# A decoder layer on one core: convolution results stored in one DMA a group, constant key rows written in the front, the loop's first tiles on other memory, two gates placed behind the convolution

## The chip, the cores and the metric

One core of a Trainium2 chip runs the whole kernel. The metric is the device time of one execution in microseconds (us): 2160.04 us, the median of three runs.

## The reference

x is 16 sequences of 512 tokens with 256 channels, the context 16 x 64 x 128. One decoder layer is three blocks, each `x = layernorm(x + block(x))`. Cut to what matters:

```python
# block 1: a gated long convolution, then a gated MLP
z = rmsnorm(u, pre_norm_w) @ in_proj_w.T                 # (16, 512, 768)
z = causal_conv3(z, short_w) + short_b                   # each channel by itself, 3 taps
x2, x1, v = split(z, 3)                                  # x2 is "the gate"
h = sum_s residues * exp(log_poles * t)                  # 256 long filters, 16 poles each
xv = x1 * v
y = (causal_conv(xv, h) + xv * D_skip) * x2
y = y @ out_proj_w.T + u
block1 = y + (gelu(rms(y) @ l1_w.T) * (rms(y) @ l2_w.T)) @ l3_w.T
# block 2: 16 heads of causal self-attention plus cross-attention to the context
block2 = (softmax(causal(q k.T)) v + softmax(qc kc.T) vc) @ Wp + bp
# block 3: a low-rank feed-forward
block3 = gelu(x @ U1 @ V1 + b1) @ U2 @ V2 + b2
```

## The kernel before

All matmuls are in float32. The kernel has two parts, each an ordered list of operations that a planner writes: `Plan.op` takes an operation with its engine, a cost, a priority, the tiles it reads and writes and the operations it must follow; `Plan.schedule` simulates the engines with those costs, picks by priority whatever can start, and `emit` writes the instructions in that order. Each engine then runs its own instructions in order, and so does the sync engine's DMA queue, which before the change issues every DMA. Buffers of a class (`"x"`: 10 tiles fx, `"row"`: 9 tiles frow, `"mm"`: the PSUM banks, ...) are given out by the same planner, and an operation that finds none waits.

**The front** (lines 362 to 920) makes what the long convolution needs of all 16 batches. `prepare(b)` loads x of a batch (L439), takes the sum of squares on ACT (L317), the inverse root on POOL (L306, L307), scales x on POOL (`scale_ops`, L330) and transposes it on PE (L344). `project(m)` is two matmuls (L469, four instructions in the trace), an activation (L476) and two multiply-adds on DVE (L484) for the three taps. `x1v(b, k)` makes two projections, multiplies them on POOL (L496), transposes the product (L502) and puts it into `xv0` or `xv1` (channels 0 to 127 and 128 to 255). `gate_of(b)` makes the two gate projections and stores them to the DRAM tensor `gates` (L518). The second half of the channels and the gates of the last nine batches come late; the gates of the last two batches (`LAST`) have the lowest priority. A transposed x stays in its fx tile until the gate of its batch is done.

The convolution then goes in eight blocks of 32 channels, four on `xv0` and four on `xv1`. A block loads four Toeplitz tiles ("toes", 512 KB each, into fx tiles, L641), which POOL cuts to a triangle (L650), and runs `near_mm` (L665), the state (L675, L685, L693), `toe_mm` (L716), ACT's exps into the single tile `far` (L701) and `far_mm` (L728). Four results of 128 x 512 are copied to rows by ACT or DVE (L297, L299) and stored to `yconv` in DRAM, each by two DMAs of 64 partitions (L746).

Weights are loaded in between, and biases and weights folded (L832, L878). The front's memory is then given to the pool `kept` of the second part. A tile of `kept` waits for whatever last used the memory it lies on (`reuse_waits="tile"`). In the order of the pool's list, `xt`, `yt`, `gate` and `y1` lie on `xv0`; `xT`, `gT` and the first rows on `xv1`; `va` lies on `far` and the first frow tiles.

**Between the two parts** POOL fills `va`, `vc`, `maxes` with constants (L958 to L971) and two row tiles are made (L966, L967) and stored into the DRAM tiles `dk` (L969): constant rows beside the keys.

**The loop** plans all 16 batches together: `first_block(b)` loads x (L1056), the gate (L1053) and the two halves of the convolution's result (`load_y`, L1047), multiplies by the gate on POOL (L1065), projects out (L1078), adds (L1028), takes the rms norm (L317, L306, L332), adds y to x on POOL (L1090), transposes (L344) and runs the MLP (L1103 onwards, L1155, additions at L1163); `attention(b)` and `ffn(b)` follow. While one batch is in attention, the next is in its MLP.

Of the kernel before, what the change touches and what calls it, by code (L numbers as in the profile page):

```python
# [8 lines left out]
F32 = mybir.dt.float32  # L9
# [7 lines left out]
P = 128  # L17
NEG = -1.0e30
HEADS = 16
# [178 lines left out]
def decoder_layer(  # L198
# [69 lines left out]
    hpad = dram.tile([D + 1, P], F32, name="hpad")  # L268
    yconv = dram.tile([NT, B, D, P], F32, name="yconv")
    gates = dram.tile([B, P, KD * T], F32, name="gates")  # L270
    normed = dram.tile([B, P, KD * T], F32, name="normed")
    weights = ctx.enter_context(tc.tile_pool(name="weights", bufs=1))
# [16 lines left out]
    def pool_(n):  # L289
        return 0.2 + n / 470.0  # L290
# [34 lines left out]
    def scale_ops(x, sq, prio, on):  # L325
        for c in range(NT):

            def fn(e, c=c):
                if e == "POOL":
                    nc.gpsimd.tensor_scalar(x.t[:, c, :], x.t[:, c, :], sq.t[:, c, 8:9], None, ALU.mult)  # L330
                else:
                    nc.scalar.activation(x.t[:, c, :], x.t[:, c, :], AF.Copy, scale=sq.t[:, c, 8:9])  # L332

            plan.op(on, pool_(D) if on == "POOL" else act(D, True), fn, prio, r=[sq], w=[(x, c)])

# [28 lines left out]
    with ExitStack() as front:  # L364
# [69 lines left out]
        def prepare(b, pr):  # L434

            x_ = View("x", lambda t: t.rearrange("p (c d) -> p c d", c=NT))
            plan.op(
                "SP", 0.5 * MB,
                lambda e: nc.sync.dma_start(out=x_.t, in_=x[b].rearrange("(c p) d -> p c d", p=P)), pr - 1000,  # L439
                w=[x_], lat=2.5, after=at_step(b - 3),  # L440
            )
            if b == 0:
                load_in(prew, pre_w, -900, [(INW, "p")])
                for k in range(KD):
                    load_in(inw[:, k, :], in_wT[bass.ts(k, P), :], -900, [(INW, k)])
                load_in(cw, conv_w, -890, [(CW, 0)])
                load_in(cb, conv_b, -890, [(CW, 1)])
                for k in range(KD):
                    plan.op(
                        "DVE", 0.9,  # L450
                        lambda e, k=k: nc.vector.tensor_scalar(
                            inw[:, k, :], inw[:, k, :], prew[:, k : k + 1], None, ALU.mult
                        ),
                        -900, r=[(INW, "p")], w=[(INW, k)],
                    )

            sq = rms_ops(x_, pr - 120)
            scale_ops(x_, sq, pr - 120, "POOL")
            xT = transposed(x_, lambda t: t, pr - 120, as_xT())
            marks.append(plan.ops[-1])  # L460
            return xT

        def project(m, xT, pr):

# [7 lines left out]

            plan.op("PE", KD * pe(T), mm, pr + 10, r=[xT, INW], w=[ps], holds=[t])
            plan.op(
# [37 lines left out]

        def gate_of(b, xT, pr):
            for m in range(KD):
                t = project(m, xT, pr)
                plan.op(
                    "SP", 0.25 * MB,
                    lambda e, m=m, t=t: nc.sync.dma_start(out=gates[b][:, bass.ts(m, T)], in_=t.t), pr,  # L518
                    r=[t], lat=2.5,
                )  # L520

        late, late_T = [], []
        for b in range(B):
# [15 lines left out]
        for b, xT in late:  # L539
# [12 lines left out]
            if b < B - LAST:  # L552
                gate_of(b, xT, 3000 + b * 100)
        for b, xT in late_T[LATE - LAST :]:
            gate_of(b, xT, 7000 + b * 100)

# [72 lines left out]
        for blk in range(NR // R8):  # L629
# [102 lines left out]

            plan.op("PE", 1.0, far_mm, pc + 10, r=[st, far], w=ys, tiling=(SLOT, P // 2))
            for c in range(HPG):
# [7 lines left out]
                )  # L742
                for par in range(2):
                    plan.op(
                        "SP", 0.6,
                        lambda e, c=c, o=o, par=par, d0=d0: nc.sync.dma_start(  # L746
                            out=yconv.rearrange("j b d t -> (j b) d t")[
                                :, d0 + c * R8 + par * R8 // 2 : d0 + c * R8 + (par + 1) * R8 // 2, :
                            ],
                            in_=o.t[bass.ts(par, 64)],  # L750
                        ),
                        pc + 10, r=[o], lat=3.0,
                    )

# [104 lines left out]
        for par in range(2):  # L859
            for rows_, col in (  # L860
# [6 lines left out]
                ones_.append(t)  # L867


        bias_p = load(bp.to_broadcast([P, D]), [P, D], "bias_p")  # L870
# [60 lines left out]
        "mm": tiles(psum, "mm", 3, [P, T]),  # L931
        "xt": tiles(kept, "xt", 5, [P, NT, D]),
        "yt": tiles(kept, "yt", 1, [P, KD, T]),
        "gate": tiles(kept, "gate", 1, [P, KD * T]),
        "y1": tiles(kept, "y1", 1, [P, NT, D]),
        "xT": tiles(kept, "xT", 3, [P, KD, T]),
        "gT": tiles(kept, "gT", 1, [P, NF, T]),
# [5 lines left out]
        "ctx2": tiles(kept, "ctx2", 2, [CC, 2, TC]),  # L943
        "va": tiles(kept, "va", 2, [P, NT, VA]),
        "vc": tiles(kept, "vc", 2, [P, HEADS // 2, SLOT]),
        "maxes": tiles(kept, "maxes", 2, [P, NT, HPG, SLOT]),
        "ex": tiles(kept, "ex", 3, [P, HPG * T]),
# [3 lines left out]
        "di": tiles(dram, "di", 2, [2 * HPG, 2, T]),  # L951
        "dk": tiles(dram, "dk", 2, [2 * HPG, SLOT, T]),
        "junk": tiles(kept, "junk", 1, [P, D]),
# [6 lines left out]
    for t in pool["vc"]:  # L960
        nc.gpsimd.memset(t, 0.0)
        nc.gpsimd.memset(t[:, :, 0:1], 1.0)

    for par in range(2):
        fixed = pool["row"][par]
        nc.gpsimd.memset(fixed, 0.0)  # L966
        nc.vector.tensor_scalar(fixed, fixed, first_rows[par], None, ALU.add)  # L967
        for t in pool["dk"]:
            nc.sync.dma_start(out=t[bass.ts(par, HPG), HD:, :], in_=fixed[0 : HPG * HD, :])  # L969
    for t in pool["maxes"]:  # L970
# [70 lines left out]
    def first_block(b, after):  # L1041
# [4 lines left out]
        def load_y(e, k):  # L1046
            nc.sync.dma_start(  # L1047
                out=yt.t[:, k, :].rearrange("p (j t) -> p j t", j=NT),
                in_=yconv[:, b, bass.ts(k, P), :].rearrange("j p t -> p j t"),
            )  # L1050
# [9 lines left out]
        for k in range(KD):  # L1060
            plan.op("SP", 0.5, lambda e, k=k: load_y(e, k), p0 - 500, w=[(yt, k)], lat=4.0)
        for k in range(KD):
            plan.op(
                "POOL", pool_(T),
                lambda e, k=k: nc.gpsimd.tensor_tensor(  # L1065
                    yt.t[:, k, :], yt.t[:, k, :], gate.t[:, bass.ts(k, T)], ALU.mult
                ),
                p0 - 100, r=[gate], w=[(yt, k)],
            )
# [16 lines left out]
        for cp in range(NT // 2):  # L1086
# [3 lines left out]
                lambda e, sl=sl: nc.gpsimd.tensor_tensor(x_.t[:, sl, :], x_.t[:, sl, :], y1.t[:, sl, :], ALU.add),  # L1090
                p0, r=[(y1, 2 * cp), (y1, 2 * cp + 1)], w=[(x_, 2 * cp), (x_, 2 * cp + 1)],
            )
# [707 lines left out]
```

## Time and profile before

| | |
|---|---|
| median of three runs (lowest, highest) | 2160.04 us (2159.8, 2162.32) |
| the profiled execution: its own time, and its span from first to last instruction | 2162.7 us, 2161.0 us |
| mean granted TensorE clock | 0.972 |
| DMA moved | 182.15 MB, mean 84 GB/s |
| DMAs in the front: yconv stores, gate stores, toes | 64 of 128 KB, 32 of 256 KB, 32 of 512 KB |

How to read it: PE, DVE, ACT and POOL are the tensor, vector, scalar and GpSimd engines; PEld is PE's weight load; SPq is the sync engine's DMA queue. A line of the timeline gives the start, the time from the first to the last of the merged instructions, engine, line, operation, output and input, their number, and in brackets the idle time before them and what ended it. A line of the windows gives a stretch, its length, the busy time of PE, PEld, DVE, ACT and POOL (with the number of instructions), the granted PE clock, the DMA share and GB/s. A line of the waits gives who waited for whom, the total, the number of times and the longest wait, in us.

### The profile page before, as it was taken

The page shows a single profiled execution, that of the slowest core. Times are in us where ns is not written, and L with a number is a line of the kernel's source. Part 1 is how long each engine was busy: PE and PEld are TensorE (multiplying, and loading weights), DVE is VectorE, ACT ScalarE, POOL GpSimd, SP SyncE. Part 2 cuts the span into 40 slices and gives each one's busy share as a digit, 9 for nine tenths or more (in the row PEclk, how much of TensorE's full clock was granted, in tenths as well). Part 3 has the DMA queues.
Part 4 walks back from the last instruction along what each step waited for, and adds up shares of the span by engine and source line. Part 5 has one row for each costly group of instructions (what it writes and reads, how often), then busy time and mean ns, then how long its engine had stood idle before and what let it go on. Part 6 is the DMA issues. An engine that isn't in the chain of part 4 may idle for free.

```text
span 2161.0 us, 35414 instructions
## 1 busy us (share of the span) xinstructions
PE 2028.3 (94%) x14324; PEld 1043.9 (48%) x14324; DVE 1342.1 (62%) x1928; ACT 941.8 (44%) x1381; POOL 720.6 (33%) x960
## 2 busy tenths in 40 slices
PE   7999949798999999999999999999999999999676
PEld 3555625444454545454545454545454545454232
DVE  5976513738384848484848484848485857575742
ACT  6863421060627161716171617161626262626243
POOL 7585432040414141414142414141414141313122
PEclk9999969899999999999999999999999999999889
DMA  5366861030304031413141313131313131212100
GB/s 177 108 203 223 260 176 49 1 109 21 110 21 125 25 119 31 119 31 119 31 118 32 117 34 114 36 114 36 113 38 110 41 96 45 76 45 75 56 10 10
DMA packets 114887, 182.15 MB, mean 84 GB/s; under 512 B 13346, under 2 KB 61987, under 8 KB 114595
## 3 DMA queue, kind: packets, MB, share of 16 engines
q1 hardware_dynamic: 114722, 179.88, 27.6%
q8 instruction: 113, 1.85, 0.4%
q14 instruction: 52, 0.42, 0.1%
HBM read 111.09 MB, written 68.76 MB: 83 GB/s over the span
## 4 chain that ended last, share of the span: by engine, by line
PE 80%; ACT 5%; DVE 4%; issue 2%; POOL 2%; DMA 1%; SPq 0%; ACTq 0%; POOLq 0%; DVEq 0%
PE mm L1103 13%; PE scores L1347 10%; PE mm L1256 8%; PE mm L1155 8%; PE scores L1425 7%; PE av L1460 7%; PE mm L1650 4%; PE av L1666 3%; PE mm L1184 3%; PE mm L1017 2%; PE fmm L469 2%; PE mm L344 2%; PE mm L1512 2%; ACT ex L1437 2%; PE scores L1486 2%
## 5 line engine op out<-in xcount | busy, mean ns | idle before, releaser
L1437 ACT ACTIVATE ex<-scores 128x2048 f32<-128x2048 f32 x160 | 300.1, 1876 | 175.5 <-PE scores L1425 172.9
L1103 PE MATMUL mm<-xT,w_l 128*128 128x512 f32 x640 | 296.6, 607 | 0.0
L1448 POOL TENSOR_SCALAR_AFFINE_SELECT ex<-ex 128x512 f32<-128x512 f32 x256 | 158.1, 635 | 381.9 <-ACT ex L1437 350.4
L1347 PE MATMUL scores<-keys,q 32*128 32x320 f32 (+4 forms) x2560 | 233.9, 472 | 42.9 <-DVE maxes L1377 18.3
L1366 DVE TENSOR_TENSOR scores<-scores,mask_qk 128x512 f32<-128x512 f32 (+1 forms) x192 | 168.3, 876 | 102.6 <-PE scores L1347 98.7
L1347 PEld LDWEIGHTS scores<-keys,q 32*128 32x128 f32 x2560 | 116.5, 191 | 179.0 <-issue 57.9
L1658 ACT ACTIVATE row<-mm,b_s 128x512 f32<-128x512 f32 x128 | 80.8, 684 | 254.0 <-PE mm L1650 253.9
L1425 PE MATMUL scores<-q,keys 32*128 32x512 f32 (+3 forms) x2048 | 183.1, 460 | 7.1 <-ACT ex L1437 7.0
L1103 PEld LDWEIGHTS mm<-xT,w_l 128*128 128x128 f32 x640 | 115.7, 190 | 146.3 <-issue 129.0
L1594 POOL TENSOR_TENSOR nd<-nd,nd 128x1024 f32<-128x1024 f32 x30 | 70.6, 2353 | 346.6 <-DMA nd<-di 346.6
L306 POOL TENSOR_SCALAR small<-small 128x4 f32<-128x4 f32 (+1 forms) x66 | 13.1, 199 | 517.2 <-DVE small L987 515.7
L1002 ACT ACTIVATE xt<-xt,small 128x256 f32<-128x256 f32 x192 | 102.7, 594 | 173.6 <-POOL small L995 144.4
L469 PE MATMUL fmm<-fx,inw 128*128 128x512 f32 x384 | 176.8, 605 | 0.0
L1460 PE MATMUL av<-ex,va 128*32 128x512 f32 (+3 forms) x2048 | 168.1, 439 | 0.0
L1115 ACT ACTIVATE row<-mm 128x512 f32<-128x512 f32 x80 | 47.8, 597 | 271.6 <-PE mm L1103 271.6
L484 DVE SCALAR_TENSOR_TENSOR frow<-fmm,cw,frow 128x511 f32<-128x511 f32 x192 | 140.6, 744 | 36.8 <-ACT frow L476 32.6
L297 DVE COPY row<-av 128x512 f32<-128x512 f32 x66 | 45.7, 692 | 184.0 <-PE av L1460 165.5
L1155 PE MATMUL mm<-w_l,gT 128*128 128x256 f32 x640 | 158.9, 384 | 0.0
L1379 DVE TENSOR_REDUCE maxes<-scores 128x4 f32<-128x2048 f32 x64 | 146.7, 2293 | 2.2
L1425 PEld LDWEIGHTS scores<-q,keys 32*128 32x128 f32 x2048 | 89.3, 183 | 104.4 <-ACT ex L1437 33.5
L1155 PEld LDWEIGHTS mm<-w_l,gT 128*128 128x128 f32 x640 | 117.9, 190 | 43.8 <-issue 30.3
L1262 DVE TENSOR_SCALAR q<-mm,bqc_s 128x512 f32<-128x512 f32 x63 | 47.3, 751 | 140.0 <-PE mm L1256 140.0
(178 smaller groups left out, 3339.8 us busy)
## 6 DMA issues: line engine op xcount, KB each, us to landing
dn<-row SPq DMA_DIRECT2D x120, 256.0 KB
fx<-hpad SPq DMA_DIRECT2D x32, 512.0 KB
keys<-dk SPq DMA_DIRECT2D x64, 256.0 KB
nd<-dn SPq DMA_DIRECT2D x30, 512.0 KB
nd<-di SPq DMA_DIRECT2D x30, 512.0 KB
fx<-in_x SPq DMA_DIRECT2D x16, 512.0 KB
gates<-frow SPq DMA_DIRECT2D x32, 256.0 KB
yconv<-frow SPq DMA_DIRECT2D x64, 128.0 KB
```

The costliest lines, as they stand in the source:

```text
L469: nc.tensor.matmul(ps.t, inw[:, k, bass.ts(m, P)], xT.t[:, k, :], start=(k == 0), stop=(k == KD - 1))
L484: lambda e, lag=lag: nc.vector.scalar_tensor_tensor(t.t[:, lag:], ps.t[:, 0 : T - lag], cw[:, m, 2 - lag : 3 - lag], t.t[:, lag:], ALU.mul ...
L1103: nc.tensor.matmul(ps.t, w[:, k, bass.ts(f, P)], zT.t[:, k, :], start=(k == 0), stop=(k == KD - 1))
L1155: nc.tensor.matmul(ps.t[:, bass.ts(cc, D)], gT.t[:, f, bass.ts(c, P)] if f < NF else gE.t, w_l3[:, f, :] if f < NF else w_l3e[:, c, :], st ...
L1256: nc.tensor.matmul(ps.t, w[:, k, cols], xT.t[:, k, :], start=(k == 0), stop=(k == KD - 1))
L1347: nc.tensor.matmul(sc.t[:, r, at : at + hi - lo], q.t[hd, bass.ts(i, P)], kk.t[hd, lo:hi], start=True, stop=True,)
L1366: nc.vector.tensor_tensor(diag, diag, mask, ALU.add)
L1379: nc.vector.tensor_reduce(own[:, 3], sc.t, AX.X, ALU.max, negate=True)
L1425: nc.tensor.matmul(sc.t[:, r, at : at + T - j * P], keys[g].t[hd, TC + j * P : TC + (j + 1) * P], qas[g].t[hd, j * P :], start=True, stop= ...
L1437: lambda e, sc=sc, ex=ex: nc.scalar.activation(ex.t.rearrange("p (r n) -> p r n", r=HPG), sc.t, AF.Exp, scale=scale),
L1448: lambda e, ex=ex, at=at: nc.gpsimd.affine_select(out=ex.t.rearrange("p (r n) -> p r n", r=HPG)[:, :, at : at + P], in_=ex.t.rearrange("p ...
L1460: nc.tensor.matmul(av[g].t[bass.ts(r, SLOT), j * P :], va.t[:, j, h * VS : h * VS + SLOT], ex.t[:, r * T + at : r * T + at + n], start=(j ...
```

## The change

- `yconv` becomes two DRAM tensors, one for each half of the channels, and each result row tile is stored by one DMA of 128 partitions instead of two of 64.
- The constant rows of `dk` are made on POOL in the front's plan and stored from there; `dk` is allocated with the other DRAM tensors. The step between the two parts is gone.
- In the pool `kept`, `va`, `vc` and `maxes` come first and `xt` goes behind `y1`. So `va`, `vc`, `maxes`, `yt`, `gate`, `y1` and the first `xt` lie on `xv0`, the other `xt` and `xT` on `xv1`, rows and queries on fx tiles, keys on the last fx tile, `far` and frow tiles.
- The gates of the last two batches are planned after the last `far_mm`, and their stores are issued by ACT's queue.
- For batch 0: x is loaded by four DMAs, scaled by DVE in the front, and multiplied by the gate on DVE in the loop.
- The gate stores of batches 0 to 3 are planned after the transposition of x of the batch two later.
- In the loop, the addition of y to x (L1090) is planned after the inverse root.

```diff
@@ -266,8 +266,10 @@
...
     hpad = dram.tile([D + 1, P], F32, name="hpad")
-    yconv = dram.tile([NT, B, D, P], F32, name="yconv")
+    yconv = [dram.tile([NT, B, P, P], F32, name=f"yconv{k}") for k in range(KD)]
     gates = dram.tile([B, P, KD * T], F32, name="gates")
+    dks = [dram.tile([2 * HPG, SLOT, T], F32, name=f"dk{n}") for n in range(2)]
     normed = dram.tile([B, P, KD * T], F32, name="normed")
@@ -326,12 +328,14 @@
...
             def fn(e, c=c):
-                if e == "POOL":
-                    nc.gpsimd.tensor_scalar(x.t[:, c, :], x.t[:, c, :], sq.t[:, c, 8:9], None, ALU.mult)
+                if e != "ACT":
+                    eng = nc.vector if e == "DVE" else nc.gpsimd
+                    eng.tensor_scalar(x.t[:, c, :], x.t[:, c, :], sq.t[:, c, 8:9], None, ALU.mult)
                 else:
...
-            plan.op(on, pool_(D) if on == "POOL" else act(D, True), fn, prio, r=[sq], w=[(x, c)])
+            cost = {"POOL": pool_(D), "DVE": dve(D), "ACT": act(D, True)}[on]
+            plan.op(on, cost, fn, prio, r=[sq], w=[(x, c)])
@@ -434,11 +438,15 @@
...
             x_ = View("x", lambda t: t.rearrange("p (c d) -> p c d", c=NT))
-            plan.op(
-                "SP", 0.5 * MB,
-                lambda e: nc.sync.dma_start(out=x_.t, in_=x[b].rearrange("(c p) d -> p c d", p=P)), pr - 1000,
-                w=[x_], lat=2.5, after=at_step(b - 3),
-            )
+            for c in range(0, NT, 1 if b == 0 else NT):
+                cs = slice(c, c + (1 if b == 0 else NT))
+                plan.op(
+                    "SP", 0.5 if b == 0 else 0.5 * MB,
+                    lambda e, cs=cs: nc.sync.dma_start(
+                        out=x_.t[:, cs, :], in_=x[b].rearrange("(c p) d -> p c d", p=P)[:, cs, :]
+                    ),
+                    pr - 1000, w=[(x_, c)] if b == 0 else [x_], lat=2.5, after=at_step(b - 3),
+                )
             if b == 0:
@@ -455,12 +463,12 @@
...
             sq = rms_ops(x_, pr - 120)
-            scale_ops(x_, sq, pr - 120, "POOL")
+            scale_ops(x_, sq, pr - 120, "POOL" if b else "DVE")
             xT = transposed(x_, lambda t: t, pr - 120, as_xT())
...
-        def project(m, xT, pr):
+        def project(m, xT, pr, after=()):
@@ -470,7 +478,7 @@
...
-            plan.op("PE", KD * pe(T), mm, pr + 10, r=[xT, INW], w=[ps], holds=[t])
+            plan.op("PE", KD * pe(T), mm, pr + 10, r=[xT, INW], w=[ps], holds=[t], after=after)
             plan.op(
@@ -510,16 +518,24 @@
...
-        def gate_of(b, xT, pr):
+        def gate_of(b, xT, pr, after=()):
             for m in range(KD):
-                t = project(m, xT, pr)
-                plan.op(
+                t = project(m, xT, pr, after)
+                if after:
+                    plan.op(
+                        "ACT", 0.6,
+                        lambda e, m=m, t=t: nc.scalar.dma_start(out=gates[b][:, bass.ts(m, T)], in_=t.t), pr,
+                        r=[t], lat=3.0,
+                    )
+                    continue
+                o = plan.op(
                     "SP", 0.25 * MB,
...
                 )
-        late, late_T = [], []
+                stores.append((b, o))
+        late, late_T, stores = [], [], []
         for b in range(B):
@@ -551,8 +567,9 @@
...
                 gate_of(b, xT, 3000 + b * 100)
+        last_gates = []
         for b, xT in late_T[LATE - LAST :]:
-            gate_of(b, xT, 7000 + b * 100)
+            last_gates.append((b, xT))
@@ -730,7 +747,7 @@
...
-            plan.op("PE", 1.0, far_mm, pc + 10, r=[st, far], w=ys, tiling=(SLOT, P // 2))
+            far_done = plan.op("PE", 1.0, far_mm, pc + 10, r=[st, far], w=ys, tiling=(SLOT, P // 2))
             for c in range(HPG):
@@ -740,17 +757,23 @@
...
                 )
-                for par in range(2):
-                    plan.op(
-                        "SP", 0.6,
-                        lambda e, c=c, o=o, par=par, d0=d0: nc.sync.dma_start(
-                            out=yconv.rearrange("j b d t -> (j b) d t")[
-                                :, d0 + c * R8 + par * R8 // 2 : d0 + c * R8 + (par + 1) * R8 // 2, :
-                            ],
-                            in_=o.t[bass.ts(par, 64)],
-                        ),
-                        pc + 10, r=[o], lat=3.0,
-                    )
+                plan.op(
+                    "SP", 0.6,
+                    lambda e, at=x0 + c * R8, kh=kh, o=o: nc.sync.dma_start(
+                        out=yconv[kh].rearrange("j b d t -> (j b) d t")[:, at : at + R8, :].rearrange(
+                            "n (h d) t -> h n (d t)", h=2),
+                        in_=o.t,
+                    ),
+                    pc + 10, r=[o], lat=3.0,
+                )
+        for b, xT in last_gates:
+            gate_of(b, xT, 7000 + b * 100, (far_done,))
+        for b, o in stores:
+            if b < 4:
+                o.deps.add(marks[b + 2])
@@ -866,6 +889,23 @@
...
+        for par in range(2):
+            fixed = Buf("row")
+            def ones_row(e, par=par, fixed=fixed):
+                nc.gpsimd.memset(fixed.t, 0.0)
+                nc.gpsimd.tensor_scalar(fixed.t, fixed.t, first_rows[par], None, ALU.add)
+            plan.op("POOL", 1.9, ones_row, 920, w=[fixed], after=at_step(5))
+            for t in dks:
+                plan.op(
+                    "SP", 0.6,
+                    lambda e, par=par, t=t, fixed=fixed: nc.sync.dma_start(
+                        out=t[bass.ts(par, HPG), HD:, :], in_=fixed.t[0 : HPG * HD, :]
+                    ),
+                    920, r=[fixed], lat=3.0,
+                )
@@ -929,10 +969,13 @@
...
         "mm": tiles(psum, "mm", 3, [P, T]),
-        "xt": tiles(kept, "xt", 5, [P, NT, D]),
+        "va": tiles(kept, "va", 2, [P, NT, VA]),
+        "vc": tiles(kept, "vc", 2, [P, HEADS // 2, SLOT]),
+        "maxes": tiles(kept, "maxes", 2, [P, NT, HPG, SLOT]),
         "yt": tiles(kept, "yt", 1, [P, KD, T]),
...
         "y1": tiles(kept, "y1", 1, [P, NT, D]),
+        "xt": tiles(kept, "xt", 5, [P, NT, D]),
         "xT": tiles(kept, "xT", 3, [P, KD, T]),
@@ -941,15 +984,12 @@
...
         "ctx2": tiles(kept, "ctx2", 2, [CC, 2, TC]),
-        "va": tiles(kept, "va", 2, [P, NT, VA]),
-        "vc": tiles(kept, "vc", 2, [P, HEADS // 2, SLOT]),
-        "maxes": tiles(kept, "maxes", 2, [P, NT, HPG, SLOT]),
         "ex": tiles(kept, "ex", 3, [P, HPG * T]),
...
         "di": tiles(dram, "di", 2, [2 * HPG, 2, T]),
-        "dk": tiles(dram, "dk", 2, [2 * HPG, SLOT, T]),
+        "dk": dks,
         "junk": tiles(kept, "junk", 1, [P, D]),
@@ -960,13 +1000,6 @@
...
         nc.gpsimd.memset(t[:, :, 0:1], 1.0)
-    for par in range(2):
-        fixed = pool["row"][par]
-        nc.gpsimd.memset(fixed, 0.0)
-        nc.vector.tensor_scalar(fixed, fixed, first_rows[par], None, ALU.add)
-        for t in pool["dk"]:
-            nc.sync.dma_start(out=t[bass.ts(par, HPG), HD:, :], in_=fixed[0 : HPG * HD, :])
     for t in pool["maxes"]:
@@ -1046,7 +1079,7 @@
...
                 out=yt.t[:, k, :].rearrange("p (j t) -> p j t", j=NT),
-                in_=yconv[:, b, bass.ts(k, P), :].rearrange("j p t -> p j t"),
+                in_=yconv[k][:, b].rearrange("j p t -> p j t"),
             )
@@ -1060,12 +1093,13 @@
...
         for k in range(KD):
-            plan.op(
-                "POOL", pool_(T),
-                lambda e, k=k: nc.gpsimd.tensor_tensor(
-                    yt.t[:, k, :], yt.t[:, k, :], gate.t[:, bass.ts(k, T)], ALU.mult
-                ),
-                p0 - 100, r=[gate], w=[(yt, k)],
+            def times_gate(e, k=k):
+                eng = nc.vector if e == "DVE" else nc.gpsimd
+                eng.tensor_tensor(yt.t[:, k, :], yt.t[:, k, :], gate.t[:, bass.ts(k, T)], ALU.mult)
+            plan.op(
+                "POOL" if b else "DVE", pool_(T) if b else dve(T), times_gate, p0 - 100, r=[gate], w=[(yt, k)]
             )
@@ -1088,7 +1122,7 @@
...
                 lambda e, sl=sl: nc.gpsimd.tensor_tensor(x_.t[:, sl, :], x_.t[:, sl, :], y1.t[:, sl, :], ALU.add),
-                p0, r=[(y1, 2 * cp), (y1, 2 * cp + 1)], w=[(x_, 2 * cp), (x_, 2 * cp + 1)],
+                p0, r=[(y1, 2 * cp), (y1, 2 * cp + 1), sq], w=[(x_, 2 * cp), (x_, 2 * cp + 1)],
             )
```

## The prediction, made before the change was run

> **What bounds the kernel now.** I read the page first, then PE's waits and the windows by stage, then the chain of waits and the sync queue's timeline where PE stands still. PE is busy 94% of the span. The loop over the 16 batches runs in steps of about 109 us in which PE idles 0.33 us (108.67 of 109.00 us busy between 886 and 995 us), so nothing that leaves PE's loop work alone can gain there. What is left is the front: PE idles for about 25 us of the first 280 us, and then stands nearly still from 280 to 316 us.
>
> ```profile
> span 2161.0 us, 35414 instructions
> PE 2028.3 (94%) x14324; PEld 1043.9 (48%) x14324; DVE 1342.1 (62%) x1928; ACT 941.8 (44%) x1381; POOL 720.6 (33%) x960
> PE   7999949798999999999999999999999999999676
> ...
> PE mm L1078 <- POOL yt L1065: 22.9, 2, 17.3
> ...
> 285.00:290.00 5.00, 0.00 (x0) 0.00 (x0) 0.00 (x0) 0.00 (x0) 0.55 (x1) 0.50 0.87 201
> 305.00:310.00 5.00, 4.42 (x12) 3.21 (x12) 1.24 (x2) 1.02 (x4) 1.27 (x1) 0.65 0.82 286
> ```
>
> In the second row of digits the sixth slice (270 to 324 us) is the hole. PE's waits from 280 to 440 us have 22.9 us at the first loop matmul (L1078), which needs yt times the gate. In the windows, PE, DVE and ACT do nothing from 285 to 290 us while DMA is busy 0.87: this stage belongs to the sync queue and the transfers. The sync queue's own timeline tells why:
>
> ```profile
> 271.01 6.84 SPq L746 DMA_DIRECT2D yconv<-frow  x8
> 277.89 0.59 SPq L518 DMA_DIRECT2D gates<-frow  x1
> 278.58 10.22 SPq L746 DMA_DIRECT2D yconv<-frow  x16
> 288.85 0.59 SPq L1056 DMA_DIRECT2D xt<-in_x  x1
> 289.48 0.55 SPq L1053 DMA_DIRECT2D gate<-gates  x1
> 290.07 0.43 SPq L1047 DMA_DIRECT2D yt<-yconv  x1
> 293.53 2.99 SPq L969 DMA_DIRECT2D dk<-row  x4
> 296.56 1.33 SPq L1047 DMA_DIRECT2D yt<-yconv  x1
> ...
> 289.45 2.05 POOL L958 MEMSET va<- 128x1152 f32 x2 [13.65 <-DMA yconv<-frow]
> ```
>
> The last far_mm ends at 279.8 us (call this T0). Sixteen stores of 128 KB are still issued until 288.8, then three loads. The second yt load stands behind the dk stores, which wait for DVE (L967), which waits for POOL's memsets, which waited 13.65 us for yconv stores, because va lay where the front's row tiles were. In the chain of waits that second load lands at 303.4; POOL's product ends at 304.7, and the MLP's matmuls (L1103) start at 316.0, T0 + 36.2.
>
> ```profile
> 9.61 0.48 PE L344 MATMUL fmm<-ident,fx 128*128 128x128 f32 x1 [9.61 <-POOL fx L330]
> 38.05 0.42 ACT L317 ACTIVATE fjunk<-fx 128x256 f32<-128x256 f32 x1 [4.69 <-DMA fx<-in_x]
> 43.71 1.12 PE L502 MATMUL fmm<-ident,frow 128*128 128x128 f32 x4 [3.43 <-POOL frow L496]
> ...
> SPq L518 <- DVE frow L484: 77.4, 15, 17.2
> ```
>
> Two smaller stalls stand at the start: PE's first instruction at 9.61 us, and PE idle 3.43 us before 43.71. The last line says that the sync queue stood up to 17.2 us at a gate store: from 10.9 to 28.1 us the load of a later batch's x (issued 28.97) queued behind it; ACT then waited 4.69 us for it, with projections behind, and PE through POOL for those.
>
> **Part by part.** The sum is made against the profiled execution: span 2161.0, its own time 2162.7 (1.7 around the span), 2.7 above the median of 2160.04.
>
> *Start of batch 0.* x in four DMAs, scaling on DVE. Removed from the path: 4 scalings on POOL of 0.92 = 3.66 us. DVE has no such row at 256 elements: the 768-element row (L451, 0.62) and the 512-element row (L967, 0.78) bound it at 0.2 to 0.4; I take 0.3, so 1.2 us. The squares, 4 x 0.54, start as the first quarter lands instead of at 4.93. Against it: three more issues of 0.45 put prew and inw 1.35 us later, and DVE scales inw first; its second half ended at 8.47, now about 9.8. x can then be scaled by about 10.5 and the projection start near 11.6 instead of 13.6. Term -2.0 (bounds -3.5 and 0).
>
> *Gate stores of batches 0 to 3 after a later transposition.* The x load no longer stands behind them. They hold their rows (9) a little longer, which costs nothing while projections find a row; if not, a projection waits a few us. The 3.43 us stall goes; next late are DVE and ACT, at 18.7 and 17.6 of 20 us between 40 and 60. Term -3.4 (bounds -5 and +2).
>
> *Key rows in the front.* Each is a memset (0.52) and an add on POOL, between the 256-element row (0.92) and the 672-element row (1.96), say 1.5: 4 us for two, wanted after batch 5's transposition, where POOL is busy 3.5 of 20 us (60 to 80). Four issues of 0.57 = 2.3 us on the sync queue among the weight loads. Term 0, covered by that slack; if they fall among POOL's work of 137 to 160 us, where it leaves hardly a gap, +4.
>
> *Last two gates behind the convolution.* Four projections of 1.72 us on PE = 6.9 us, 4 x 0.78 on ACT, 8 x 0.75 on DVE. They were not all on the path: at 244 to 250 us they fill PE while the last x1v goes through ACT, DVE and POOL. That product ended at 246.1, its transposition came at 247.61 behind eight of their instructions and the copy 0.3 later: term -1.7 (bounds -6.9 and 0). Two fx tiles of ten stay taken, so eight of the second half's sixteen toes instead of six are loaded after the convolution has begun; toes landed there 1.6 us apart (selects at 260.43 to 265.21), so +3.2 at worst. But the last toe (issued 267.25) stood behind eight stores of 5.82 us, now four. I take +1.0 (bounds -3 and +5).
>
> *One store a group, and the passage to the loop.* A 256 KB store of 128 rows is not there to yconv; gates<-frow (same size and rows) took 0.33 median, yconv's 128 KB 0.58. Four a block: 1.3 to 2.3 us instead of 4.95 to 6.84. From T0: first copy 0.7, four stores at 0.58 to +3.1, xt, gate and first yt to +4.7. The second yt waits only for the last store, landing unknown: between 1 us and the yt load's 5.55, I take 3, issue at +6.1. dk, its DVE and POOL work and the memsets' wait are gone from here (va now lies on xv0). Bytes set the landing: about 1 MB of stores, 1 MB of xt and gate, 0.5 MB of yt and some 0.75 MB of the moved gate stores at the 250 GB/s that a share of 0.86 at 213 GB/s makes: 13 us, landing near +14. Without the gate stores +10.5; with all of them ahead and poorer packing +18. DVE multiplies in 0.7 (L1028's 0.69) instead of 1.26: +14.8 against +24.9. From there 11.3 us to the MLP, now 11.1, since rsqrt no longer stands behind the addition of L1090 (0.2). Term -10.3 (bounds -14 and -6). The moved projections end at about +7 and DVE with them near +10, inside this gap: that work is hidden by the loads, and would cost up to 3 us if the loads came at once.
>
> On the moved stores the row is the DMA share, 0.86 to 0.87 from 280 to 295 us: already full. The Trainium skill (DMA: Bandwidth & Descriptors, Issuing engines are not separate DMA queues) says that another issuing engine saves sequencer time only and the transfers still share the same 16 engines; by it the ACT queue buys nothing here, and were all four stores free instead, the landing would be the +10.5 above. On the clock the row is 0.50 granted at 285 to 300 us and 0.65 at 305 to 310, where 12 matmuls of L1078 took 4.69 us (16 took 3.45 at 356 us). The skill (TensorE: Matmul & The Clock Gate, Why this matters for your kernels) wants no idle gap above about 3 us; by it the moved projections, ending at +7, don't keep the clock up until +14.8; if they did, 2 us more would be gained.
>
> *Loop.* The new order in POOL (rsqrt before the two additions, 2 x 1.27) holds in all batches. PE waits 0.33 us a batch; additions are needed only at L1163's additions some 70 us later. Term 0, with 3 either way for a rearranged plan.
>
> Sum: -2.0 - 3.4 + 0 - 1.7 + 1.0 - 10.3 = -16.4. On the profiled time 2146.3; on the median's scale 2143.6.
>
> **Rivals.** *Front gains lost*: the convolution is set by toes and eight slots, so whatever comes earlier waits there (DMA share 0.72 to 0.94 from 240 to 270 us speaks for it; the far tile's chain of copies and exps, 269 to 280 us, against). Then about -10, less if stores crowd the yt load: 2148 to 2155. *All better*: the gates were wholly on PE's path and the landing is early: 2130 to 2137. *Loop slower*: the additions now fall among POOL's selects of ex (L1448), which PE's av matmuls (L1460) await. The price is at most 2 x 1.27 = 2.5 us a batch, 15 batches, 38 us: about 2182. It decides from 16.4/15 = 1.1 us a batch on. Against it: POOL is a third busy, and the list of operations is reordered around it. *It doesn't do what it says*: load_g or load_y waits for the ACT stores too, since they share the gates tensor; then loads go at about +12, landing +18 to +20, and -5 to -9 in all remains: 2151 to 2155. The first yt load at 290.07, which started 1.3 us after the last yconv issue without a wait, speaks against whole-tensor waits.
>
> **How the numbers follow.** Forecast (2137 to 2148) 0.60; front gains lost 0.17; all better 0.08; shared-tensor waits 0.07; slower loop 0.08. Leaving out the slower loop and the very ends gives 2131 to 2155. A measurement of this kernel tells about 0.2% (4.3 us) from no change, so faster means below 2155.7: 0.60 + 0.16 + 0.08 + 0.04 = 0.88; same 0.06 (the rivals' weak ends and a loop near its threshold), slower 0.06.
>
> **What would show it.** After the last far_mm: four yconv issues instead of sixteen, no dk stores, second yt issue within 7 us, landing by +14, L1078 waiting some 10 us less. PE's first L469 near 11.6 us, and no 3.4 us stall near 43 us. The loop's step still 109 us, PE idle below 0.5. Wrong would be: a step above 110 us, toes awaited by POOL for more than now (18.8 us between 180 and 320 us), or the yt loads landing later than +18.

## The result, and the profile after: 2276.64 us, slower

The changed kernel takes 2276.64 us (median of four runs, 2275.41 to 2280.16) against 2161.18 us for the kernel before beside it. The ratio is 1.0535 with a 95% interval of 1.0517 to 1.0554. The forecast was 2143.6 us, the range 2131 to 2155, and 0.06 stood on slower. The profiled execution took 2276.77 us with a span of 2275.1 us, 114.1 us more than the span before.

The head of the page shows where it is not: the loop.

```profile
span 2275.1 us, 35425 instructions
...
PE 2041.8 (90%) x14324; PEld 1050.2 (46%) x14324; DVE 1347.7 (59%) x1927; ACT 943.4 (41%) x1386; POOL 716.7 (32%) x956
...
PE   8996552698989999999999999999999999999776
...
DMA  5363251310312223131313040404041312121200
```

The fourth to eighth slices of PE (171 to 455 us) stand at 6, 5, 5, 2 and 6 tenths (9, 9, 4, 9 and 7 before), and the DMA row under them at 3, 2, 5, 1 and 3: PE waits while most DMA engines are idle. Split at three marks (start of the second half's `near_mm`, end of the last `far_mm`, start of the MLP), the 114.1 us are 56.4 before the first mark (249.9 to 306.3 us), 16.5 in the second half of the convolution (29.9 to 46.4 long), 39.6 in the passage from there to the MLP (36.2 to 75.8 long) and 1.6 in all the rest. The sync queue's timeline shows what fills them:

```profile
190.52 9.84 SPq L762 DMA_DIRECT2D yconv<-frow  x4
...
207.03 17.65 SPq L762 DMA_DIRECT2D yconv<-frow  x4
224.79 7.89 SPq L658 DMA_DIRECT2D fx<-hpad  x5
...
318.56 9.94 SPq L762 DMA_DIRECT2D yconv<-frow  x4
328.61 6.28 SPq L658 DMA_DIRECT2D fx<-hpad  x3
334.97 61.44 SPq L762 DMA_DIRECT2D yconv<-frow  x12
396.46 4.96 SPq L1089 DMA_DIRECT2D xt<-in_x  x1
...
404.57 5.54 SPq L1080 DMA_DIRECT2D yt<-yconv  x2
```

L762 is the new store (L746 before), L658 the toes (L641 before). Before, sixteen stores of 128 KB took 10.22 us of the queue; now twelve of 256 KB take 61.44, or 5.12 each. 256 KB in 5.12 us is 51 GB/s. The yconv tile's answer gives the issues of all 32 (minimum, median and maximum in ns); in the trace they add up to 122.8 us, against 39.4 us for the 64 issues before. The windows, in a stretch where nothing but these stores moves, say why. A line of the windows ends with the clock, the DMA share and GB/s:

```profile
L762 SPq DMA_DIRECT2D yconv<-frow x32: 491/4949/6562, 190.5 to 391.0; - x32
```

```profile
360.00:365.00 5.00, 0.00 (x0) 0.00 (x0) 0.00 (x0) 1.27 (x2) 0.00 (x0) 0.97 0.13 51
...
886.00:995.00 109.00, 108.67 (x752) 54.70 (x752) 72.11 (x101) 47.58 (x63) 33.85 (x46) 1.00 0.25 74
```

A share of 0.13 of sixteen engines is two engines, at some 25 GB/s each. The last line is the loop's step: 108.67 busy of 109.00 us, as before. The waits from 180 to 430 us (who waited for whom, us in total, times, longest) show who stood behind the stores:

```profile
POOL fx L667 <- DMA fx<-hpad: 74.7, 19, 18.6
...
PE mm L1112 <- DVE yt L1099: 54.5, 1, 54.5
...
ACT frow L484 <- DMA yconv<-frow: 48.6, 10, 9.0
```

The first: POOL's cut of a toe waits for its load, which is queued behind stores on the sync queue (18.8 us in all from 180 to 320 us before). The second is the first loop matmul (22.9 us in two waits before). The third was not there before: ACT waits for a row tile that a store is still reading.

### The profile page after: what moved, and what is told of

Read it like the earlier page. It is cut to its first block, busy times and chain, and to the rows that moved or that the text cites. A ratio compares the mean times of both kernels' runs of the same rounds, so it can differ in the third digit from the quotient of the medians.

```text
span 2275.1 us, 35425 instructions
## 1 busy us (share of the span) xinstructions
PE 2041.8 (90%) x14324; PEld 1050.2 (46%) x14324; DVE 1347.7 (59%) x1927; ACT 943.4 (41%) x1386; POOL 716.7 (32%) x956
## 4 chain that ended last, share of the span: by engine, by line
PE 77%; DMA 6%; DVE 5%; ACT 5%; POOL 3%; SPq 2%; issue 2%; ACTq 0%; POOLq 0%; DVEq 0%
PE mm L1137 13%; PE scores L1381 9%; PE mm L1290 8%; PE mm L1189 7%; PE scores L1459 7%; PE av L1494 7%; DMA yconv<-frow 4%; PE mm L1684 4%; PE av L1700 3%; PE mm L1218 3%; PE mm L1050 2%; PE fmm L477 2%; ACT ex L1471 2%; PE mm L348 2%; PE mm L1546 2%
## 5 line engine op out<-in xcount | busy, mean ns | idle before, releaser
L1381 PE MATMUL scores<-keys,q 32*128 32x320 f32 (+4 forms) x2560 | 233.2, 471 | 39.4 <-DVE maxes L1408 15.6
L477 PE MATMUL fmm<-fx,inw 128*128 128x512 f32 x384 | 178.2, 608 | 4.1 <-DVE xv L299 1.4
```

Source lines behind the costliest of these rows:

```text
L477: nc.tensor.matmul(ps.t, inw[:, k, bass.ts(m, P)], xT.t[:, k, :], start=(k == 0), stop=(k == KD - 1))
L1381: nc.tensor.matmul(sc.t[:, r, at : at + hi - lo], q.t[hd, bass.ts(i, P)], kk.t[hd, lo:hi], start=True, stop=True,)
```

## The experiments

The first theory (A in the expectations) was the shape of the store's destination. The store writes `h n (d t)`, that is 2 x 64 x 512 elements: its outermost dimension counts 2. The pair before wrote 64 x 512 each. The rivals were that one of the other edits did it, or that a store of 128 rows is slow for another reason than its outermost dimension. The second theory was that the two fx tiles held for the late gates starve the toes of slots: B in the expectations where it stands for the whole loss, D where it stands for what is left without the one store. All times below come from the profiled execution of each kernel, in us; the median and the ratio to the kernel before come from the timed runs. How far two profiled executions of the same work differ can be read from e6 and e10: their edit is in the loop, and all engines run the same instructions in the same order up to the end of the convolution, which still ends at 276.8 us in one and at 280.0 in the other. A difference of up to some 3 us between two rows of the first three columns can therefore not be taken for an effect by itself.

| kernel | second half starts | last far_mm ends | MLP starts | span | median | ratio (95%) |
|---|---|---|---|---|---|---|
| before | 249.9 | 279.8 | 316.0 | 2161.0 | 2161.18 to 2162.55 | |
| after | 306.3 | 352.7 | 428.4 | 2275.1 | 2276.64 | 1.0535 (1.0517 to 1.0554) |
| e2: before, one store | 308.8 | 355.2 | 431.4 | 2277.2 | 2279.04 | 1.0541 (1.0526 to 1.0557) |
| e1: after, two stores | 247.8 | 288.8 | 318.7 | 2164.6 | 2171.22 | 1.0045 (1.0028 to 1.0062) |
| e4: two stores, outermost 4 | 271.0 | 326.9 | 364.9 | 2211.5 | 2213.52 | 1.0236 (1.0221 to 1.0252) |
| e5: two stores, outermost 8 | 248.8 | 294.7 | 326.9 | 2172.8 | 2174.80 | 1.0060 (1.0045 to 1.0075) |
| e7: before, front edits | 248.4 | 277.7 | 315.9 | 2161.1 | 2162.77 | 1.0002 (0.9994 to 1.0011) |
| e8: passage edits, two stores | 251.6 | 284.2 | 313.2 | 2158.8 | 2159.28 | 0.9986 (0.9977 to 0.9995) |
| e9: before, late gates | 247.6 | 288.6 | 332.9 | 2178.2 | 2181.31 | 1.0093 (1.0079 to 1.0107) |
| e6: e1, gates back in front | 247.5 | 276.8 | 306.7 | 2151.9 | 2156.04 | 0.9977 (0.9968 to 0.9986) |
| e12: e1, late gates reload x | 247.7 | 276.6 | 310.3 | 2157.2 | 2158.66 | 0.9983 (0.9974 to 0.9992) |
| e10: e6, additions free | 249.8 | 280.0 | 308.5 | 2153.6 | 2154.88 | 0.9967 (0.9954 to 0.9980) |
| e11: e10, half the stores on ACT | 254.1 | 289.2 | 314.8 | 2160.2 | 2160.40 | 0.9986 (0.9977 to 0.9995) |

### The store alone, and everything but the store

e2 puts the one store into the kernel before; e1 puts the two stores back into the changed one.

```diff
 e2, on the kernel before
-                for par in range(2):
...
+                        out=yconv.rearrange("j b d t -> (j b) d t")[:, d0 + c * R8 : d0 + (c + 1) * R8, :].rearrange(
+                            "n (h d) t -> h n (d t)", h=2),
+                        in_=o.t,
 e1, on the changed kernel
+                for par in range(2):
...
+                            out=yconv[kh].rearrange("j b d t -> (j b) d t")[:, at : at + R8 // 2, :],
+                            in_=o.t[bass.ts(par, 64)],
```

> The kernel before with one edit: each result row tile is stored by a single DMA whose destination is walked as 2 x 64 x 512; nothing else is changed. Theory A: 32 stores at 5.1 us instead of 64 at 0.58 hold the sync queue about 127 us longer, nearly all of it on the path: 2265 to 2300 us. Theories B and C: none of their causes is here, so 2150 to 2165.

> The changed kernel with one edit: each result row tile is stored by two DMAs of 64 partitions again, to the same two yconv tensors. Theory A (the one store walks its destination as 2 x 64 x 512 and is carried by two of the sixteen DMA engines: twelve of them took 61.4 us to issue at the end of the front, 5.1 us each, 51 GB/s): the whole loss goes, and what I forecast of the rest comes, 2143 to 2152 us. Theory B (the two fx tiles held for the last gates starve the toe loads: POOL waits 74.7 us for toes between 180 and 430 us, against 18.8 before): stays slow, above 2230. Theory C (the stores on ACT's queue, the other layout in memory or the new order in the loop): stays slow too.

e2 measured 2279.04 us, as slow as the whole change and as theory A expected; e1 measured 2171.22. The store alone makes the loss, and nothing else in the change is needed for it. In e2 no late gates run beside the stores, so a long stretch holds stores and nothing else:

```profile
365.00:370.00 5.00, 0.00 (x0) 0.00 (x0) 0.00 (x0) 0.00 (x0) 0.00 (x0) 0.50 0.13 51
```

What is left of the change in e1 is still no gain: 2171.22 is 9.3 us above the kernel before, where 2143 to 2152 was expected. The rest of the experiments is about that.

### The outermost dimension by itself

e4 and e5 keep two stores of 64 partitions and 128 KB, as in e1, and change only the way that the destination is divided. `yconv` gets one batch more than it needs for each outer index, so that the dimensions cannot be joined: 4 x 16 x 512 in e4, 8 x 8 x 512 in e5.

```diff
 e4
+    yconv = [dram.tile([NT * 1, B // 1 + 1, P, P], F32, name=f"yconv{k}") for k in range(KD)]
...
+                            out=yconv[kh][:, 0 : B // 1, at : at + R8 // 2, :].rearrange("m b d t -> m b (d t)"),
+                            in_=o.t[bass.ts(par, 64)],
 e5: the same with NT * 2 and B // 2
```

> As e1, but yconv has one unused sequence row after every 16, so that each 64-partition store walks its destination as 4 x 16 x 512 instead of 64 x 512; bytes, number of stores and loads are those of e1. Theory A (as many DMA engines as the outermost dimension, 25.6 GB/s each): 128 KB on four engines is 1.28 us a store, 10.2 us a block instead of 4.6: some 20 to 45 us above e1, 2165 to 2195. If it is the 128 partitions or the 256 KB of one DMA that are slow: as e1, within 4 us.

> As e4 with one unused row after every 8, so that each store walks 8 x 8 x 512. Theory A: eight engines, 0.64 us a store, about what one issue takes (0.58): within 8 us of e1, not faster. If it isn't the outermost dimension: as e1.

e4 measured 2213.52 us, 42.3 above e1: the 20 to 45 that were expected, though above 2165 to 2195, which counted on a faster e1. Its second half starts 23.1 us later than e1's and takes 55.9 us instead of 40.9. e5 measured 2174.80, 3.6 us above e1, which both theories allow, so for it the DMA share has to decide. Bytes, partitions, rows of 2 KB and number of DMAs are those of e1; only the outer count differs, and the load of yt steps over the unused batches. Stretches of e4 (first line), e5 (second) and the kernel before (third) in which stores move alone:

```profile
308.00:310.00 2.00, 0.00 (x0) 0.00 (x0) 0.00 (x0) 0.00 (x0) 0.00 (x0) 0.50 0.26 103
```

```profile
282.00:284.00 2.00, 0.00 (x0) 0.00 (x0) 0.00 (x0) 0.00 (x0) 0.84 (x1) 0.50 0.52 188
```

```profile
284.00:286.00 2.00, 0.00 (x0) 0.00 (x0) 0.00 (x0) 0.00 (x0) 0.00 (x0) 0.50 0.87 204
```

So an outer count of 2, 4 and 8 keeps 0.13, 0.26 and 0.52 of the engines busy, which is 2, 4 and 8 of sixteen, and moves 51, 103 and 188 GB/s; the count of 64 before ran at a share of 0.87 and 204 GB/s. From 8 to 64 the share thus grows much more than the rate; what holds the rate there was not tried. The Trainium skill (DMA: Bandwidth & Descriptors, Why a DMA increments its semaphore by 16 and not by 1) has this rule: a DMA is divided over the largest number of engines, up to sixteen, that divides the outermost dimension above 1 of both sides. The shares of all four shapes here agree with it. The same page (Rules for kernel authors) advises one transfer of 128 partitions instead of two of halves, since both halves already use all engines; here that merging alone cost 117 us (e2), because the two halves could be put into one destination only with the 2 outermost.

### The front edits alone, and the passage edits alone

e7 is the kernel before with x of batch 0 in four DMAs, its scaling on DVE and the later gate stores of batches 0 to 3. e8 is the changed kernel with two stores, without these three and with the gates in front: memory order, key rows in front, gate times yt on DVE, additions after the root.

```diff
 e7, on the kernel before
+            for c in range(0, NT, 1 if b == 0 else NT):
...
+            scale_ops(x_, sq, pr - 120, "POOL" if b else "DVE")
...
+        for b, o in stores:
+            if b < 4:
+                o.deps.add(marks[b + 2])
 e8, on e6: these three taken out
```

> The kernel before with the front's edits alone: x of batch 0 in four DMAs and scaled by DVE, gate stores of batches 0 to 3 planned later. My forecast: -2.0 and -3.4, 2156.5. Rival: in e1 PE started 2.9 us earlier and the 3.4 us stall near 43 us was gone, but PE lost 2.1 us at 40 to 60 and 2.7 us at 60 to 80 us to ACT and DVE, which were the next to be late; then 0 to -2 remains.

> The passage alone: key rows set up in the front, va, vc, maxes and yt on xv0, batch 0's product with the gate on DVE, additions after the inverse root, yconv as two tensors, with two stores a row tile; the front's start and the gates as before. My forecast of this term was -10.3 with one store a row tile; with two, the sync queue is busy to about T0 + 9 as before, so some 3 us less: -7, 2153 to 2157. If the loop's new order costs, the batch step shows it.

e7 measured no difference, where 5.4 us had been forecast. Its convolution ends 2.1 us earlier (277.7 against 279.8), and its sync queue is through with the yconv stores 2.2 us earlier (at 286.6 instead of 288.8). But the dk stores and the second yt load of e7's sync queue are where they were, 293.53 and 296.56 before:

```profile
281.67 4.93 SPq L753 DMA_DIRECT2D yconv<-frow  x8
...
293.55 3.02 SPq L980 DMA_DIRECT2D dk<-row  x4
296.61 1.15 SPq L1058 DMA_DIRECT2D yt<-yconv  x1
```

In e7 POOL's memset of `va` waits 15.0 us for yconv stores instead of 13.7 and so starts only 0.9 us earlier, at 288.54; and the two additions on DVE behind it (L978), which make the rows that the dk stores carry, take 3.06 us instead of 1.49. Between the two the gain is gone. e8 removes the wait and gains 2.3 us in the median, where 2153 to 2157, about 7 us, was expected: 7.2 less in the passage (29.0 instead of 36.2), 4.4 of it given back since the convolution ends later. Whether an edit makes it end later (the key rows, the other memory) was not separated, and e6 and e10 differ by 3.2 us there without one. With both sets of edits in e6 the front shows: 3.2 us less than e8 in the median of eleven runs each.

### The late gates

e9 is the kernel before with only the late gates on ACT's queue; e6 is e1 with them in front again; e12 is e1 with the late gates, but x of the last two batches is stored in DRAM as that of other late batches and loaded again after the convolution, so that no fx tile is held.

```diff
 e9, on the kernel before: gate_of(b, xT, 7000 + b * 100, (far_done,)) after the blocks
 e6, on e1
-            last_gates.append((b, xT))
+            gate_of(b, xT, 7000 + b * 100)
 e12, on e1
-                if b < B - KEPT:
+                if b < B - KEPT or b >= B - LAST:
...
+            again = as_xT()
...
+                7000 + b * 100, r=[(NORMED, b)], w=[again], lat=2.5, after=(far_done,),
+            gate_of(b, again, 7000 + b * 100, (far_done,))
```

> The kernel before with the last two batches' gates behind the last far_mm, stored by ACT's queue, alone. My forecast: -1.7 + 1.0, so 2159 to 2162. Theory D: the convolution's second half takes 11 us longer: +5 to +12, 2166 to 2173.

> e1 (the changed kernel with two stores a row tile) with the last two batches' gates back in front of the convolution, stored by the sync queue. In e1 the passage from the first of the last four blocks' near_mm to the last far_mm took 40.9 us (247.8 to 288.75) against 29.9 before. Theory D (the two fx tiles held for the late gates cost those 11 us: the last three toes are issued one at a time between stores at 265, 273 and 279 us): that stretch falls back to 30 to 32 us and the kernel is 6 to 11 us faster than e1, 2158 to 2165. Theory E (the split yconv, the front's dk work or the order of the front costs it): as e1.

> e1 (late gates, two stores a row tile) with the transposed x of the last two batches put into DRAM and loaded again after the last far_mm, so that their two fx tiles are free for toes; the gates stay late. Theory D (the held tiles make the convolution's second half 11 us longer): first near_mm to last far_mm is back at 29 to 32 us. What it costs after that, two loads of 512 KB before the gates, is extra. Theory F (the late gates' order or the missing work on PE stretches it, not the tiles): the stretch stays at 38 to 41 us.

The late gates cost 20 us alone (2181.31) and 15 us in the change (2171.22 against 2156.04), more than the 5 to 12 and 6 to 11 that were expected. The second half of the convolution takes 41.0 us in e9, 40.9 in e1, 29.3 in e6 and 28.9 in e12, which has late gates and no held tile. That settles the larger part, some 12 us: its price is the two tiles. (e12 is still 2.6 us above e6. Its passage, with the loads and the gates in it, takes 33.7 us instead of 29.9.) The sync queue of e1, with POOL's select and PE's Toeplitz matmul behind one of its toes:

```profile
265.14 1.55 SPq L658 DMA_DIRECT2D fx<-hpad  x1
267.75 5.47 SPq L763 DMA_DIRECT2D yconv<-frow  x8
273.33 0.52 SPq L658 DMA_DIRECT2D fx<-hpad  x1
273.95 5.13 SPq L763 DMA_DIRECT2D yconv<-frow  x8
279.19 0.53 SPq L658 DMA_DIRECT2D fx<-hpad  x1
```

```profile
278.03 1.09 POOL L667 TENSOR_SCALAR_AFFINE_SELECT fx<-fx 128x1024 f32<-128x1024 f32 x1 [5.51 <-DMA fx<-hpad]
```

```profile
279.18 1.97 PE L733 MATMUL fmm<-fx,xv 128*64 128x128 f32 x16 [6.02 <-POOL fx L667]
```

The last three toes of the block chain are issued one by one, between groups of eight stores. With eight tiles in circulation they wait for a tile and, in the list's order, behind eight stores; PE then waits 6.02 us for one and 3.68 for the next. Nor does moving the gates away gain anything in front: the second half starts at 247.8 us in e1 and at 247.5 in e6.

e9 loses 4.5 us more than e1 does against e6. In it POOL's memset of `va` comes at 306.16 us instead of 289.45, and the dk stores and the second yt load behind it (296.56 before):

```profile
306.16 2.06 POOL L967 MEMSET va<- 128x1152 f32 x2 [21.51 <-issue]
```

```profile
310.24 2.99 SPq L978 DMA_DIRECT2D dk<-row  x4
313.28 0.99 SPq L1056 DMA_DIRECT2D yt<-yconv  x1
```

The profile does not name what the memset waited for. In the kernel before `va` lies on `far` and row tiles, which the late gates use until they are stored; that this is the wait was not tried.

### The additions, and stores on ACT's queue

e10 takes back the edit that plans L1124 (L1090 before) after the inverse root. e11 then gives every second yconv store to ACT's queue.

```diff
 e10, on e6
-                p0, r=[(y1, 2 * cp), (y1, 2 * cp + 1), sq], w=[(x_, 2 * cp), (x_, 2 * cp + 1)],
+                p0, r=[(y1, 2 * cp), (y1, 2 * cp + 1)], w=[(x_, 2 * cp), (x_, 2 * cp + 1)],
 e11, on e10
+                        "ACT" if par else "SP", 0.35 if par else 0.6,
...
+                        (nc.scalar if par else nc.sync).dma_start(
```

> e6 without the new order in the loop (the addition of y to x no longer planned after the inverse root). In e6 the MLP starts 13.5 us after the first out projection, against 11.3 before: ACT's scaling of y waits 2.7 us for the additions, which still read y. If that is the cause, the first batch's MLP starts 2 to 2.5 us earlier after L1112 and the kernel takes 2151 to 2155; if the order matters in every batch, the step changes too. My forecast had put this edit at a gain of 0.2: then it would be slower by that.

> e10 with the second of the two stores of each row tile issued by ACT's queue instead of the sync queue: four issues a block on each, sixteen DMA engines for each store. This is what the one-DMA store was meant to give the sync queue. In e6 the sync queue ends its stores 8.7 us after the last far_mm. If issue time is the limit there, it ends at about +4 and the first out projection comes 3 to 4 us earlier: 2147 to 2152. If the transfers are the limit (DMA share 0.86), as e10. If ACT's exps for the far tile are held up by its waits for DVE's copies, the convolution gets longer: up to +5.

e10 is the fastest kernel here, 2154.88 us, within what was expected, though 1.2 us below e6 is less than these runs resolve. In its trace ACT's scaling of y (L335) no longer waits for the additions; first e6, then e10:

```profile
303.22 0.91 ACT L335 ACTIVATE y<-y,small 128x256 f32<-128x256 f32 x2 [2.69 <-POOL xt L1124]
```

```profile
305.45 1.71 ACT L335 ACTIVATE y<-y,small 128x256 f32<-128x256 f32 x4 [1.65 <-POOL small L309]
```

From the end of the first sixteen L1112 matmuls to the MLP e10 takes 6.5 us and e6 8.0. All kernels here that have this edit take 8.0 us there, all others 6.5, the kernel before too: the edit costs 1.5 us, less than the 2 to 2.5 that were expected. It costs them once: from the MLP's start to the end e6 and e10 take 1845.3 and 1845.1 us.

e11 is slower than e10 by 5.5 us, and the profile shows a gain and a larger loss. After the last far_mm the sync queue is through with its stores in 3.2 us (8.1 in e10), and the first L1112 starts 12.4 us after that far_mm (15.6 in e10): that is what was expected if the time of the issues is the limit. How much of it the second queue gave, and how much the longer convolution, which left no older stores in the queue, was not separated. The loss is in front of that: the second half starts 4.3 us later (254.1 against 249.8) and takes 35.1 us instead of 30.2. PE waits 3.92 us for ACT's exps, which stand behind ACT's copies and stores. The first line below shows the sync queue's last twelve stores. It runs over 16.10 us because the queue waits for copies in between: an issue takes 0.54 us in the median of e11's 32 on this queue, and from 288 to 290 us no DMA moves anything.

```profile
276.26 16.10 SPq L763 DMA_DIRECT2D yconv<-frow  x12
```

```profile
286.12 0.70 PE L745 MATMUL fmm<-far,state 16*64 16x128 f32 x8 [3.92 <-ACT far L718]
```

## Why the prediction was wrong, step by step

**One store a group: the step that failed.** It priced four stores of 256 KB at 1.3 to 2.3 us from rows of the same size and partitions (gates<-frow, 0.33; yconv, 0.58). Both have a destination whose outermost dimension is 128 or 64. Four of the new ones take 9.84 to 17.65 us, and all 32 hold the queue for 122.8 us. No row that it used had an outermost dimension of 2, and the working did not look at the shape, only at bytes and rows; its bounds should have come from there. The consequence was not confined to the passage, as the term had it: stores of the first half delay the toes of the same queue, 56.4 of the 114.1 us.

**The passage without the store.** Predicted -10.3; with two stores the passage is 36.2 - 29.0 = 7.2 us shorter in e8 and 6.3 in e6. In e6 the second product with the gate ends 17.1 us after the last far_mm (predicted 14.8, before 24.9), and the MLP follows 12.8 later (predicted 11.1, before 11.3). The landing's mechanism and most of its size held, though with sixteen stores instead of four. The tail failed: the additions that were meant to make room by 0.2 us cost 1.5, since ACT's scaling of y waits for them.

**The last two gates.** Predicted -1.7 + 1.0 with bounds of -3 to +5 on the tiles; measured +15 in the change and +20 alone. The working had seen the toes wait for slots, but took one late toe of 3.2 us and then subtracted the halved stores. The gates had been free filling where they were: front term 0 instead of -1.7.

**The front.** Predicted -5.4. Step by step it did what it said: L477 (L469 before) starts at 10.68 instead of 13.59 us, and the 3.43 us stall near 43 us is gone. "Next late are DVE and ACT" was true to a larger degree than priced: PE is busy for 16.64 us of 60 to 80, where it was full before, so the stall has moved on. 2.1 us reach the end of the convolution in e7, no more than two profiled executions can differ by there, and none the end of the kernel. With the passage changed too the front's edits are worth 3.2 us. The rival "front gains lost" had the right result for them alone and the wrong place: not the toes, but the wait of `va` and the additions on DVE behind it.

**Key rows, loop.** The key rows take 4.2 us of POOL (2 x 0.52 + 2 x 1.57), as estimated; whether they cost e8 its later start stays open. The loop term of 0 held (in all kernels here the time from the MLP's start to the end is 1845 to 1847 us), and so the rival that ended slower, POOL's additions in the loop, fell.

**ACT's queue.** The prediction weighed what the Trainium skill says (DMA: Bandwidth & Descriptors, Issuing engines are not separate DMA queues): another issuing engine saves issue time only. e11 fits it, with 3.2 us less from the last far_mm to the out projection, but does not test it alone, and ACT's waits made it a loss.

## What to carry to other kernels

Before two DMAs are merged, write down both access patterns and look at the outermost dimension, not at bytes and partitions: a 2 there left fourteen of sixteen engines idle. A slow store on a queue shared with loads costs most where the loads are awaited, which can be far from the store. Work that seems to be in the way on the busiest engine may be filling a gap, and moving it keeps its inputs alive: count the buffers that it holds before counting the time that it frees. And before a difference of 2 or 3 us between two profiles is explained, find two profiles of the same work and see how far they differ.

## What the runs showed of the hardware that was not expected

- A DMA's engines follow its outermost count: 2, 4 and 8 gave 51, 103 and 188 GB/s at shares of 0.13, 0.26 and 0.52, some 23 to 26 GB/s an engine; 64 gave 204 GB/s at 0.87.
- A store that the engines cannot take holds the issuing queue itself: the issue of 256 KB took 0.49 us at best and 4.95 in the median, about its transfer's own time at 51 GB/s, so that everything behind it on the queue waits as well. The hold comes early: of the stores from 318.56 us on, after a stretch without any, the first two took 0.49 us each to issue, the third 3.93 and the fourth 4.73.
- PE's gaps are paid a second time through the clock: the 128 `near_mm` matmuls that open the second half took 1.57 us in e6, with the gates in front of them and a granted clock of 1.00, and 2.79 in e1, after PE had stood idle for 3.95 and 1.23 us, at a granted clock of 0.50.
